# The head of an attention stage: statistics split over two engines, the first pair prepared earlier, input blocks in borrowed memory

## Chip, core and metric

The kernel runs on one core of one Trainium2 chip. The metric is device time in microseconds (us) for one execution; the time before is the median of three runs. TensorE is PE in the profile, VectorE DVE, ScalarE ACT, GpSimd POOL, SyncE SP (it issues nearly all DMAs of the part looked at here).

## The reference, cut to what matters

An image x of 256 x 256 pixels with 128 channels (fp32) goes through two residual layers. Only the first is touched by the change:

```python
def _gn(v, G=32, eps=1e-5):                      # group norm: 32 groups of 4 channels,
    g = v.reshape(B_, H_, W_, G, C_ // G)        # mean and variance over all pixels
    m = jnp.mean(g, axis=(1, 2, 4), keepdims=True)
    s = jnp.var(g, axis=(1, 2, 4), keepdims=True)
    return ((g - m) / jnp.sqrt(s + eps)).reshape(v.shape)

q = split_heads(einsum(_gn(x), wq)) / sqrt(32)   # 4 heads of 32, in each of the 256 rows
k, v = split_heads(einsum(kv_x, wk)), split_heads(einsum(kv_x, wv))
a = softmax(q @ k + bias1 + bias2)
o = (a @ v) * sigmoid(einsum(_gn(x), wg) + bg)
x = x + einsum(o, wo) + bo
# layer 1: x = x + spectral convolutions and attention over channels of _gn(x)
```

The group norm needs all of x before the first query can be made. Keys and values come from kv_x and need no norm.

## The kernel before, in words

The first stage of `layer0` reads x in 32 blocks of 1 MB (`xb`, L129 to L136). A block has 128 partitions of 16 pixels, 128 channels each. PE transposes it in four groups of four 128x128 pieces into a PSUM tile (tag "a", six buffers), and `bn_stats` on DVE writes six numbers per channel and group into `stats`. The blocks have four SBUF buffers, so SP issues the load of block b when PE has read block b - 4. SP's DMAs are issued in program order: a load that has to wait holds all that stand behind it. Eight DMA semaphores are used in turn, so a DMA also waits for the one eight places before it to have landed.

After block 2 come the constants: `gavg` (a matrix that averages 4 channels), `bg`, `adft` and the five weight matrices. These are read through a tile with two buffers (tag "w"), transposed by PE and copied by ACT into `wT`. In SP's program the third weight, `w_wv`, stands behind block 3, and `w_wo` behind block 4. In PE's program the five weight transposes stand between block 2 and block 3. After block 8, `rows.prepare` loads and transposes the two biases (ACT takes the exp, POOL scales it). After the last block, `rows.load(0)` and `rows.load(1)` bring the first two pairs of rows of x and kv_x (`xk`; a pair takes eight DMAs of 64 KB in 128-byte pieces).

Then comes the serial chain. `bn_aggr` (L156) folds all 128 sets of statistics into a mean and a variance per channel, `group_stats` averages over groups with two small matmuls and ends in `rsqrt` (add, ACT's Sqrt, reciprocal and one Newton step), and `rows.fold` scales wq and wg by the norm's factor and makes the biases `qb` and `hbg`.

`rows.run` then does the 256 rows of attention. Its compute and its DMAs are in an order written out by hand, in pairs of rows g: `turn` transposes a pair on DVE (L293), `project` makes queries and keys of a row (PE, then ACT adds `qb`, L308), `values` makes values and the gate's input of a pair, `gates` is the gate's tanh on ACT (L323), `scores` is q times k (L333) and the first two exps (L342), `weigh` multiplies by exp(bias1) on DVE (L354) and POOL (L359) and adds halves on POOL (L364), `attend` applies it to the values. `out` and `spectrum` finish a pair, the latter writing the spectra into U. U is a large SBUF tile, 128 x 129 x 256, allocated from the beginning of the kernel; before the first `spectrum` only its first 2048 elements of a partition are in use, as the landing place of bias1.

Pools are stacked: `rows.run` opens its pools after the first stage's pools have closed, and takes over their SBUF and PSUM.

Of the kernel before, what the change touches and what calls it, by code (L numbers as in the profile page):

```python
# [10 lines left out]
FP = mybir.dt.float32  # L11
AF = mybir.ActivationFunctionType
ALU = mybir.AluOpType
# [83 lines left out]
def layer0(tc, I, C, ident, x1d, U, Q2, mv2, groups):  # L97

    nc = tc.nc
    x = I["x"][0]
    NS = x.shape[0]
    with ExitStack() as ctx:
        const = ctx.enter_context(tc.tile_pool(name="l0c", bufs=1))  # L110
        rctx = ctx.enter_context(ExitStack())
        wT = {}
        mr = const.tile([P, 2], FP, name="mr1")
        bg = const.tile([P, 1], FP, name="bg")

        bad = const.tile([P, 2, 8], FP, name="bad")
        onec = const.tile([P, 1], FP, name="onec")
        nc.vector.memset(onec, 1.0)
        adft = const.tile([P, 2, 129], FP, name="adft")

        rows = Rows(tc, I, rctx, x1d, U, Q2, mv2, wT, bg, adft, bad, ident)
        with tc.tile_pool(name="l0p", bufs=2) as pp, tc.tile_pool(
            name="l0pp", bufs=6, space=PSUM
        ) as ps_p:
            gavg = pp.tile([P, P], FP, name="gavg", bufs=1)
            stats = pp.tile([P, NS // 2, 6], FP, name="stats1", bufs=1)

            xr = x.rearrange("s q c -> (s q) c").rearrange("(b p n) c -> b p n c", p=P, n=16)
            for b in range(xr.shape[0]):  # L129
                xb = pp.tile([P, 16, P], FP, tag="xb", name=f"xb_{b}", bufs=4)  # L130
                nc.sync.dma_start(xb, xr[b])
                for t in range(4):
                    ps = ps_p.tile([P, 512], FP, tag="a", name=f"xps_{b}_{t}")
                    for k in range(4):
                        nc.tensor.transpose(ps[:, k * P : (k + 1) * P], xb[:, 4 * t + k, :], ident)
                    nc.vector.bn_stats(stats[:, b * 4 + t, :], ps)  # L136
                if b == 2:
                    nc.sync.dma_start(gavg, C["gavg"])
                    nc.sync.dma_start(bg, I["L0_conv_bg"].unsqueeze(1))
                    nc.sync.dma_start(adft, C["adft"].rearrange("(j p) f -> p j f", p=P))  # L140
                    for n in ("wq", "wk", "wv", "wg", "wo"):
                        w = pp.tile([P, P], FP, tag="w", name="w_" + n)
                        nc.sync.dma_start(w, I["L0_conv_" + n])
                        ps = ps_p.tile([P, 512], FP, tag="a", name="wps_" + n)
                        nc.tensor.transpose(ps[:, 0:P], w, ident)
                        wT[n] = const.tile([P, P], FP, name="wT_" + n)
                        if n in ("wq", "wo"):
                            nc.scalar.mul(wT[n], ps[:, 0:P], WO_SCALE if n == "wo" else 1.0 / math.sqrt(32.0))
                        else:
                            nc.scalar.copy(wT[n], ps[:, 0:P])  # L150
                if b == 8:
                    rows.prepare(pp, ps_p)
            rows.load(0)
            rows.load(1)
            mv = pp.tile([P, 2], FP, name="mv1", bufs=1)
            nc.vector.bn_aggr(mv, stats.rearrange("p a b -> p (a b)"))  # L156
            g = group_stats(nc, pp, ps_p, mv, gavg, "g1")
            nc.vector.tensor_copy(mr, g)
            rows.fold(ps_p, mr)

        rows.run()
        rctx.close()

        with tc.tile_pool(name="l0f", bufs=1) as fp, tc.tile_pool(
            name="l0fp", bufs=1, space=PSUM
        ) as ps_f, tc.tile_pool(name="l0fg", bufs=1, space=PSUM) as ps_g:
            groups.load(fp)
            f = fp.tile([P, 3], FP, name="f")
# [12 lines left out]
            again = nc.values_load(fi[0:1, 0:1])  # L181
            groups.make(fp, ps_g, mv2, "g2")
            with tc.If(again > 0):
                layer0_general(tc, I, ident, x1d, U, Q2, wT, mr, bg, adft)
                for k in range(8):
                    row_sums(nc, U, Q2, mv2, k)
                groups.make(fp, ps_g, mv2, "g3")
# [9 lines left out]
class Rows:  # L197
# [20 lines left out]
        self.b2T = const.tile([P, 2, self.NS], FP, name="b2T")  # L218
        self.rows, self.raw = {}, {}

    def fold(self, psum, mr):

        nc = self.tc.nc
        nc.vector.tensor_scalar(self.nm, mr[:, 0:1], -1.0, None, ALU.mult)
        ps = psum.tile([P, 512], FP, tag="a", name="foldps")
        for k, n in enumerate(("wq", "wg")):
            nc.vector.tensor_scalar(self.wn[n], self.wT[n], mr[:, 1:2], None, ALU.mult)
            nc.tensor.matmul(ps[:, k : k + 1], self.wn[n], self.nm, start=True, stop=True)
        nc.vector.tensor_copy(self.qb, ps[:, 0:1])
        nc.vector.tensor_scalar(self.hbg, ps[:, 1:2], self.bg, 0.5, ALU.add, ALU.mult)  # L230

    def prepare(self, bp, ps_b):
        nc, I, ident = self.tc.nc, self.I, self.ident
# [36 lines left out]
    def run(self):  # L270
# [1 line left out]
        nc = tc.nc  # L272
        ctx, wT, rows, raw = self.ctx, self.wT, self.rows, self.raw
        b1T, b2T, bad = self.b1T, self.b2T, self.bad
        wk = ctx.enter_context(tc.tile_pool(name="l0wk", bufs=2))
        ps_s = ctx.enter_context(tc.tile_pool(name="l0s", bufs=1, space=PSUM))
        ps_a = ctx.enter_context(tc.tile_pool(name="l0a", bufs=4, space=PSUM))
        pairs = {}
        turned = wk.tile([P, 6, 512], FP, name="turned", bufs=1)

        def by_columns(out, w, src, start=True, stop=True):

            for h in range(4):
                hd = slice(32 * h, 32 * h + 32)
                nc.tensor.matmul(out[hd], w[:, hd], src, start=start, stop=stop)  # L285
# [4 lines left out]
        def turn(g):  # L290
# [6 lines left out]
            if g + 2 < NS // 2:  # L297
                self.load(g + 2)

        def project(s):  # L300
            p, q = row(s)
            ps = ps_a.tile([P, 512], FP, tag="a", name=f"qk_{s}")
            by_columns(ps[:, 0:256], self.wn["wq"], p["xT"][:, q])
            by_columns(ps[:, 256:512], wT["wk"], p["kvT"][:, q])
            r = rows[s] = {}
            r["qkT"] = wk.tile([P, 512], FP, tag="qkT", name=f"qkT_{s}")

            nc.scalar.activation(r["qkT"], ps, AF.Identity, bias=self.qb)  # L308

        def values(g):  # L310
            p = pairs[g]
            ps = ps_a.tile([P, 512], FP, tag="a", name=f"v_{g}")
            for c in range(4):
                by_columns(ps[:, c * P : (c + 1) * P], p["kvT"][:, c * P : (c + 1) * P], wT["wv"])
            p["v"] = wk.tile([P, 4, P], FP, tag="v", name=f"v_{g}")
            nc.scalar.copy(p["v"].rearrange("p c d -> p (c d)"), ps)
            p["g"] = ps_a.tile([P, 512], FP, tag="a", name=f"g_{g}")
            by_columns(p["g"], self.wn["wg"], p["xT"])

# [104 lines left out]
        def whole(k):  # L424
            return 0 <= k < NS // 2

        with tc.manual_schedule(engines={ENG.PE, ENG.Activation, ENG.DVE, ENG.Pool, ENG.SP}):
            turn(0)
            for i in range(-1, NS + 5):
                g, odd = i // 2, i % 2  # L430
                if odd and whole(g - 2):
                    again(g - 2)
                    squares(g - 2)
                if not odd and whole(g):
                    gates(g)
                if 0 <= i < NS:
                    scores(i)
# [2 lines left out]
                if 0 <= i < NS:  # L440
                    exp = rows[i].pop("exp")
                    exp(1, 0)
                    exp(1, 1)
                    weigh(i)
                if odd and whole(g + 1):
                    values(g + 1)
                if odd and whole(g + 2):
                    turn(g + 2)
                if not odd and whole(g - 2):
# [1684 lines left out]
```

## Time and profile before

| | us |
|---|---|
| median of 3 runs | 2658.32 (2653.32 to 2668.18) |
| the profiled execution | 2673.89, span 2672.1 |
| end of the last `bn_stats` in the span | 102.4 |
| first product with exp(bias1) on DVE, on POOL | 122.0, 123.8 |
| the rows of attention | about 123.8 to 1436 |
| layer 1 | the rest, to 2672.1 |

A line of the timeline gives the start, the length, the engine, the line of the kernel, the operation with output and inputs, how many were merged, and in brackets how long the engine sat idle before and what released it. In tables of windows, each engine's busy time stands in the window, then the granted PE clock (1.00 is full), the share of the DMA engines in use, and the bytes moved.

### The profile page before, as it was taken

The page shows a single profiled execution, that of the slowest core. Times are in us where ns is not written, and L with a number is a line of the kernel's source. Part 1 is how long each engine was busy: PE and PEld are TensorE (multiplying, and loading weights), DVE is VectorE, ACT ScalarE, POOL GpSimd, SP SyncE. Part 2 cuts the span into 40 slices and gives each one's busy share as a digit, 9 for nine tenths or more (in the row PEclk, how much of TensorE's full clock was granted, in tenths as well). Part 3 has the DMA queues.
Part 4 walks back from the last instruction along what each step waited for, and adds up shares of the span by engine and source line. Part 5 has one row for each costly group of instructions (what it writes and reads, how often), then busy time and mean ns, then how long its engine had stood idle before and what let it go on. Part 6 is the DMA issues. An engine that isn't in the chain of part 4 may idle for free. (4 is left out here: it accounts for less than half of the span.)

```text
span 2672.1 us, 88760 instructions
## 1 busy us (share of the span) xinstructions
PE 2426.5 (91%) x37572; PEld 1549.0 (58%) x37572; DVE 2027.5 (76%) x2886; ACT 1421.3 (53%) x2718; POOL 1488.8 (56%) x1042
## 2 busy tenths in 40 slices
PE   6699999999999999999997999998979978898754
PEld 6555655555656555565554567786755456444533
DVE  6799999999999999999996457566546654465455
ACT  0278888888888888888884122001016401555232
POOL 1199999999999999999994012002136411111211
PEclk8899999999999999999998989999989988899855
DMA  9755666556566666565652011888877764997598
GB/s 348 222 91 100 107 105 107 101 104 105 105 105 109 107 107 108 102 106 103 109 101 63 4 58 47 274 272 289 297 264 265 239 223 149 332 359 260 192 386 344
DMA packets 1017925, 459.02 MB, mean 172 GB/s; under 512 B 831094, under 2 KB 947273, under 8 KB 1011128
## 3 DMA queue, kind: packets, MB, share of 16 engines
q1 hardware_dynamic: 977720, 363.13, 54.1%
q0 software_dynamic: 22912, 81.80, 7.9%
q10 hardware_dynamic: 16896, 8.39, 1.1%
q8 instruction: 298, 4.88, 0.8%
q14 instruction: 99, 0.81, 0.1%
HBM read 317.89 MB, written 135.27 MB: 170 GB/s over the span
## 5 line engine op out<-in xcount | busy, mean ns | idle before, releaser
L359 POOL TENSOR_TENSOR e<-e,b1T 128x1024 f32<-128x1024 f32 x256 | 607.1, 2372 | 143.8 <-DMA xk<-in_x_dram 76.2
L364 POOL TENSOR_TENSOR es<-e 128x512 f32<-128x512 f32 x512 | 648.4, 1289 | 0.0
L386 DVE RECIPROCAL av<-av 128x256 f32<-128x256 f32 x256 | 452.1, 1766 | 9.1
L342 ACT ACTIVATE sc<-sc,b2T 128x512 f32<-128x512 f32 x512 | 338.7, 662 | 122.9 <-PE sc L333 110.8
L342 ACT ACTIVATE e<-sc,b2T 128x512 f32<-128x512 f32 x512 | 324.7, 694 | 0.0
L354 DVE TENSOR_TENSOR e<-sc,b1T 128x1024 f32<-128x1024 f32 x256 | 310.9, 1215 | 9.7 <-ACT sc L342 9.3
L333 PE MATMUL sc<-qkT 32*128 32x256 f32 x4096 | 293.9, 400 | 3.4 <-DVE e L354 3.4
L1392 PE MATMUL yps<-xt,mpT 128*128 128x256 f32 x1024 | 252.8, 398 | 29.2 <-DVE yt L1404 12.6
L374 PE MATMUL av<-e,v 128*32 128x256 f32 x4096 | 269.1, 379 | 1.8 <-DVE gate L387 1.7
L333 PEld LDWEIGHTS sc<-qkT 32*128 32x128 f32 x4096 | 185.5, 184 | 115.2 <-issue 53.0
L1392 PEld LDWEIGHTS yps<-xt,mpT 128*128 128x128 f32 x1024 | 195.7, 197 | 75.4 <-DVE yt L1404 18.7
L374 PEld LDWEIGHTS av<-e,v 128*32 128x32 f32 x4096 | 130.0, 109 | 126.1 <-issue 38.3
L1408 POOL DMA_DIRECT2D yd<-yt x32 | 17.5, 546 | 320.2 <-DVE yt L1404 317.5
L308 ACT ACTIVATE qkT<-qk,qb 128x512 f32<-128x512 f32 x256 | 174.4, 681 | 7.5 <-PE qk L285 7.5
L285 PEld LDWEIGHTS u<-adft,x 128*32 128x32 f32 x4096 | 120.6, 111 | 82.7 <-issue 78.6
L285 PE MATMUL qk<-turned,wn_wq 128*32 128x256 f32 x2048 | 164.5, 393 | 1.8 <-DVE turned L293 1.8
L410 ACT ACTIVATE turned<-turned 128x256 f32<-128x256 f32 x256 | 104.4, 408 | 113.7 <-DVE x1b L396 111.4
L379 PE MATMUL av<-es,ones 128*32 128x256 f32 x2048 | 161.1, 379 | 1.6 <-POOL es L364 1.6
L285 PE MATMUL qk<-turned,wT_wk 128*32 128x256 f32 x2048 | 158.4, 381 | 0.0
L293 DVE STREAM_TRANSPOSE turned<-xk 128x1024 f32<-128x1024 f32 x128 | 157.9, 1234 | 0.1
L1795 ACT ACTIVATE blocks<-h2ps,col 128x512 f32<-128x512 f32 x128 | 88.9, 777 | 128.3 <-PE h2ps L1259 128.3
L285 PE MATMUL u<-adft,x 128*32 128x129 f32 x4096 | 139.5, 276 | 6.2 <-DMA x<-x1d 6.2
(532 smaller groups left out, 4177.7 us busy)
## 6 DMA issues: line engine op xcount, KB each, us to landing
xt<-x1d SPq DMA_DIRECT2D x128, 512.0 KB, 7.8
xb<-in_x_dram SPq DMA_DIRECT2D x32, 1024.0 KB, 7.8
xk<-in_x_dram SPq DMA_DIRECT2D x512, 64.0 KB, 3.1
xk<-in_L_conv_kv_x_dram SPq DMA_DIRECT2D x512, 64.0 KB, 2.5
x1d<-x1b SPq DMA_DIRECT2D x512, 64.0 KB, 2.2
x<-x1d SPq DMA_DIRECT2D x128, 256.0 KB, 3.2
y<-yd SPq DMA_DIRECT2D x62, 512.0 KB, 6.3
gs<-Gd SPq DMA_DIRECT2D x384, 64.0 KB, 5.3
```

What stands on the lines that cost most here:

```text
L285: nc.tensor.matmul(out[hd], w[:, hd], src, start=start, stop=stop)
L293: nc.vector.transpose(turned[:, a : b + 1 : b - a].rearrange("p k (b c) -> p k b c", c=32), t)
L308: nc.scalar.activation(r["qkT"], ps, AF.Identity, bias=self.qb)
L333: nc.tensor.matmul(sc[h // 2][:, h % 2, c * 256 : (c + 1) * 256], qkT[p, 256 + c * P : 256 + (c + 1) * P], qkT[p, 0:256], start=True, stop ...
L342: nc.scalar.activation(r["e"][1][:, :, c, :] if hp else z, z, AF.Exp, bias=b2T[:, c, s : s + 1])
L354: nc.vector.tensor_tensor(r["e"][0].rearrange("p h c q -> p (h c q)"), r.pop("sc").rearrange("p h x -> p (h x)"), b1T[:, 0:2].rearrange("p ...
L359: nc.gpsimd.tensor_tensor(e1, e1, b1T[:, 2:4].rearrange("p h c q -> p (h c q)"), ALU.mult)
L364: nc.gpsimd.tensor_tensor(es, e[:, :, 0, :], e[:, :, 1, :], ALU.add)
L374: nc.tensor.matmul(ps[hd, 0:256], p["v"][:, 2 * (s % 2) + c, hd], r["e"][h // 2][:, h % 2, c, :], start=(c == 0), stop=(c == 1),)
L379: nc.tensor.matmul(ps[32 * h : 32 * h + 32, 256:512], self.ones, r["es"][h // 2][:, h % 2, :], start=True, stop=True,)
L386: nc.vector.reciprocal(rd, rd)
L1392: nc.tensor.matmul(rows_of(ps[j]), mpT[:, sc, tt], by_turn(xt[:, sc])[:, j], start=(sc == 0), stop=False,)
```

## The change

- `Rows.run` becomes a generator in four steps. Its pool for `turned`, `qkT` and `v` and its PSUM pool of four banks are opened ahead of the first stage, whose PSUM buffers go from six to four.
- The blocks of x land in U (five places behind the bias) instead of a pool with four buffers.
- After block 29, ACT sums the statistics of the first 30 blocks (the means shifted by the first one, their squares, and the second moments) with three activations, and a Sqrt of one column follows on ACT. POOL makes mean and variance of them with six small operations. `gavg` becomes two matrices, weighted by the blocks' shares 30/32 and 2/32, scaled by POOL after block 2.
- `bn_aggr` takes the last two blocks only. The two averaging matmuls become two pairs, accumulating in PSUM. DVE reads PSUM itself where ACT made a copy.
- `turn(0)` and the keys of row 0 stand between the second averaging matmul and `rsqrt`; row 0's query stands between the fold of wq and that of wg. The values of pair 0 follow, and the gate's matmuls and tanh of pair 0 move behind the exps of row 0.
- In every row, the keys' four matmuls now stand ahead of the queries' four.

```diff
         rows = Rows(tc, I, rctx, x1d, U, Q2, mv2, wT, bg, adft, bad, ident)
+        steps = rows.run()
+        next(steps)
         with tc.tile_pool(name="l0p", bufs=2) as pp, tc.tile_pool(
-            name="l0pp", bufs=6, space=PSUM
+            name="l0pp", bufs=4, space=PSUM
         ) as ps_p:
-            gavg = pp.tile([P, P], FP, name="gavg", bufs=1)
+            gavg = pp.tile([P, 2, P], FP, name="gavg", bufs=1)
...
+            room = U.rearrange("p f s -> p (f s)")
...
-                xb = pp.tile([P, 16, P], FP, tag="xb", name=f"xb_{b}", bufs=4)
+                xb = room[:, 2048 * (1 + b % 5) : 2048 * (2 + b % 5)].rearrange("p (n c) -> p n c", c=P)
                 nc.sync.dma_start(xb, xr[b])
...
+                    for k, share in ((1, late / NB), (0, 1 - late / NB)):
+                        nc.gpsimd.tensor_scalar(gavg[:, k], gavg[:, 0], share, None, ALU.mult)
...
+                if b == NB - late - 1:
+                    early = stats[:, 0 : 4 * (b + 1)].rearrange("p b (h k) -> p (b h) k", h=2)
+                    n, flat = 8 * (b + 1), junk[:, 0 : 8 * (b + 1)]
+                    nc.gpsimd.tensor_scalar(col[:, 6:7], early[:, 0, 1:2], -1.0, None, ALU.mult)
+                    nc.scalar.activation(flat, early[:, :, 1], AF.Identity, bias=col[:, 6:7], accum_out=col[:, 7:8])
+                    nc.scalar.activation(
+                        flat, early[:, :, 1], AF.Square, bias=col[:, 6:7], accum_out=col[:, 8:9]
+                    )
+                    nc.scalar.activation(flat, early[:, :, 2], AF.Identity, accum_out=col[:, 9:10])
+                    nc.scalar.activation(col[:, 10:11], col[:, 9:10], AF.Sqrt)
+                    g = nc.gpsimd
+                    g.tensor_scalar(col[:, 7:9], col[:, 7:9], 1.0 / n, None, ALU.mult)
...
             rows.load(0)
             rows.load(1)
-            mv = pp.tile([P, 2], FP, name="mv1", bufs=1)
-            nc.vector.bn_aggr(mv, stats.rearrange("p a b -> p (a b)"))
-            g = group_stats(nc, pp, ps_p, mv, gavg, "g1")
-            nc.vector.tensor_copy(mr, g)
-            rows.fold(ps_p, mr)
-
-        rows.run()
+
+            last = pp.tile([P, 2], FP, name="mv1", bufs=1)
+            with tc.manual_schedule(engines={ENG.PE, ENG.Activation, ENG.DVE, ENG.Pool}):
+                nc.vector.bn_aggr(last, stats[:, 4 * (NB - late) :].rearrange("p a b -> p (a b)"))
+                nc.vector.tensor_copy(col[:, 1:4:2], last)
+                ps = ps_p.tile([P, 512], FP, tag="a", name="g1_ps")
+                for k in range(2):
+                    nc.tensor.matmul(ps[:, 0:1], gavg[:, k], col[:, k : k + 1], start=(k == 0), stop=(k == 1))
+                nc.vector.tensor_copy(mr[:, 0:1], ps[:, 0:1])
+                d = col[:, 4:6]
+                nc.vector.tensor_scalar(d, col[:, 0:2], mr[:, 0:1], None, ALU.subtract)
+                nc.vector.tensor_mul(d, d, d)
+                nc.vector.tensor_add(d, d, col[:, 2:4])
+                ps = ps_p.tile([P, 512], FP, tag="a", name="g1_ps2")
+                for k in range(2):
+                    nc.tensor.matmul(ps[:, 0:1], gavg[:, k], d[:, k : k + 1], start=(k == 0), stop=(k == 1))
+                next(steps)
+                rsqrt(nc, pp, mr[:, 1:2], ps[:, 0:1], EPS, "g1")
+                ps = ps_p.tile([P, 512], FP, tag="a", name="foldps")
+                rows.fold(ps, mr, "wq")
+                next(steps)
+                rows.fold(ps, mr, "wg")
+
+        for _ in steps:
+            pass
...
+        def keys(s):
+            p, q = row(s)
+            ps = ps_a.tile([P, 512], FP, tag="a", name=f"qk_{s}")
+            rows[s] = {"qk": ps}
+            by_columns(ps[:, 256:512], wT["wk"], p["kvT"][:, q])
...
+        yield
+        turn(0)
+        keys(0)
+        yield
+        project(0)
+        yield
+        wk = ctx.enter_context(tc.tile_pool(name="l0wk", bufs=2))
+        ps_s = ctx.enter_context(tc.tile_pool(name="l0s", bufs=1, space=PSUM))
         with tc.manual_schedule(engines={ENG.PE, ENG.Activation, ENG.DVE, ENG.Pool, ENG.SP}):
-            turn(0)
-            for i in range(-1, NS + 5):
+            values(0)
+            turn(1)
+            for i in range(0, NS + 5):
...
+                if i == 0:
+                    gate(0)
+                    gates(0)
```

`fold` now does one of its two weights per call, and `gate` holds the gate's matmuls that `values` had; both are otherwise as before.

More of the change, by code (lines that the diff above doesn't have):

```diff
@@ L121, in layer0 @@
         rows = Rows(tc, I, rctx, x1d, U, Q2, mv2, wT, bg, adft, bad, ident)
+        steps = rows.run()
+        next(steps)
         with tc.tile_pool(name="l0p", bufs=2) as pp, tc.tile_pool(
-            name="l0pp", bufs=6, space=PSUM
+            name="l0pp", bufs=4, space=PSUM
         ) as ps_p:
-            gavg = pp.tile([P, P], FP, name="gavg", bufs=1)
+            gavg = pp.tile([P, 2, P], FP, name="gavg", bufs=1)
             stats = pp.tile([P, NS // 2, 6], FP, name="stats1", bufs=1)
+            col = pp.tile([P, 12], FP, name="col1", bufs=1)
+            junk = pp.tile([P, NS], FP, name="junk1", bufs=1)
+            room = U.rearrange("p f s -> p (f s)")
             xr = x.rearrange("s q c -> (s q) c").rearrange("(b p n) c -> b p n c", p=P, n=16)
-            for b in range(xr.shape[0]):
-                xb = pp.tile([P, 16, P], FP, tag="xb", name=f"xb_{b}", bufs=4)
+            NB, late = xr.shape[0], 2
+            for b in range(NB):
+                xb = room[:, 2048 * (1 + b % 5) : 2048 * (2 + b % 5)].rearrange("p (n c) -> p n c", c=P)
                 nc.sync.dma_start(xb, xr[b])
@@ L137, in layer0 @@
                 if b == 2:
-                    nc.sync.dma_start(gavg, C["gavg"])
+                    nc.sync.dma_start(gavg[:, 0], C["gavg"])
                     nc.sync.dma_start(bg, I["L0_conv_bg"].unsqueeze(1))
@@ L150, in layer0 @@
                             nc.scalar.copy(wT[n], ps[:, 0:P])
+                    for k, share in ((1, late / NB), (0, 1 - late / NB)):
+                        nc.gpsimd.tensor_scalar(gavg[:, k], gavg[:, 0], share, None, ALU.mult)
                 if b == 8:
                     rows.prepare(pp, ps_p)
+                if b == NB - late - 1:
[10 more added lines that the diff above has]
+                    g.tensor_scalar(col[:, 7:9], col[:, 7:9], 1.0 / n, None, ALU.mult)
+                    g.tensor_tensor(col[:, 0:1], col[:, 7:8], col[:, 6:7], ALU.subtract)
+                    g.tensor_tensor(col[:, 7:8], col[:, 7:8], col[:, 7:8], ALU.mult)
+                    g.tensor_scalar(col[:, 9:10], col[:, 9:10], 1.0 / (256 * n), None, ALU.mult)
+                    g.tensor_tensor(col[:, 8:9], col[:, 8:9], col[:, 7:8], ALU.subtract)
+                    g.tensor_tensor(col[:, 2:3], col[:, 8:9], col[:, 9:10], ALU.add)
@@ L219, in __init__, with fold @@
         self.rows, self.raw = {}, {}
-    def fold(self, psum, mr):
+    def fold(self, ps, mr, n):
         nc = self.tc.nc
[L224 to L230, printed above, removed]
+        nc.vector.tensor_scalar(self.wn[n], self.wT[n], mr[:, 1:2], None, ALU.mult)
+        if n == "wq":
+            nc.vector.tensor_scalar(self.nm, mr[:, 0:1], -1.0, None, ALU.mult)
+            nc.tensor.matmul(ps[:, 0:1], self.wn[n], self.nm, start=True, stop=True)
+            nc.vector.tensor_copy(self.qb, ps[:, 0:1])
+        else:
+            nc.tensor.matmul(ps[:, 1:2], self.wn[n], self.nm, start=True, stop=True)
+            nc.vector.tensor_scalar(self.hbg, ps[:, 1:2], self.bg, 0.5, ALU.add, ALU.mult)
     def prepare(self, bp, ps_b):
@@ L274, in run @@
         b1T, b2T, bad = self.b1T, self.b2T, self.bad
-        wk = ctx.enter_context(tc.tile_pool(name="l0wk", bufs=2))
-        ps_s = ctx.enter_context(tc.tile_pool(name="l0s", bufs=1, space=PSUM))
+        first = ctx.enter_context(tc.tile_pool(name="l0w1", bufs=2))
         ps_a = ctx.enter_context(tc.tile_pool(name="l0a", bufs=4, space=PSUM))
         pairs = {}
-        turned = wk.tile([P, 6, 512], FP, name="turned", bufs=1)
+        turned = first.tile([P, 6, 512], FP, name="turned", bufs=1)
         def by_columns(out, w, src, start=True, stop=True):
@@ L298, in turn @@
                 self.load(g + 2)
+        def keys(s):
[3 more added lines that the diff above has]
+            by_columns(ps[:, 256:512], wT["wk"], p["kvT"][:, q])
         def project(s):
             p, q = row(s)
-            ps = ps_a.tile([P, 512], FP, tag="a", name=f"qk_{s}")
+            if s not in rows:
+                keys(s)
+            r = rows[s]
+            ps = r.pop("qk")
             by_columns(ps[:, 0:256], self.wn["wq"], p["xT"][:, q])
-            by_columns(ps[:, 256:512], wT["wk"], p["kvT"][:, q])
-            r = rows[s] = {}
-            r["qkT"] = wk.tile([P, 512], FP, tag="qkT", name=f"qkT_{s}")
+            r["qkT"] = first.tile([P, 512], FP, tag="qkT", name=f"qkT_{s}")
             nc.scalar.activation(r["qkT"], ps, AF.Identity, bias=self.qb)
@@ L314, in values, with gate @@
                 by_columns(ps[:, c * P : (c + 1) * P], p["kvT"][:, c * P : (c + 1) * P], wT["wv"])
-            p["v"] = wk.tile([P, 4, P], FP, tag="v", name=f"v_{g}")
+            p["v"] = first.tile([P, 4, P], FP, tag="v", name=f"v_{g}")
             nc.scalar.copy(p["v"].rearrange("p c d -> p (c d)"), ps)
+        def gate(g):
+            p = pairs[g]
             p["g"] = ps_a.tile([P, 512], FP, tag="a", name=f"g_{g}")
@@ L433, in run @@
                     squares(g - 2)
-                if not odd and whole(g):
+                if not odd and whole(g) and g > 0:
                     gates(g)
@@ L444, in run @@
                     weigh(i)
+                if i == 0:
+                    gate(0)
+                    gates(0)
                 if odd and whole(g + 1):
                     values(g + 1)
+                    gate(g + 1)
                 if odd and whole(g + 2):
```

## The prediction

> **What bounds the kernel now.** First the page, for where the change lies: its last edit acts in the rows of attention, all others before the first POOL product at 123.8 us of the span.
>
> ```profile
> span 2672.1 us, 88760 instructions
> ...
> PE   6699999999999999999997999998979978898754
> ...
> DMA  9755666556566666565652011888877764997598
> ```
>
> A slice is 66.8 us. In slices 3 to 21 PE is at 9 and the DMA at 5 or 6: the rows are bound by engines, and their table of windows (123.8 to 1436) gives PE 1307.9 of 1312.2 us, DVE 1266.7, POOL 1244.1, that is 5.1 us a row. Only the first two slices can get shorter, and the rows just start sooner if their rate stays. Second, the windows of the first stage:
>
> ```profile
> 10.00:15.00 5.00, 3.06 (x25) 2.52 (x23) 4.56 (x8) 0.04 (x1) 0.00 (x0) 1.00 0.75 263
> 15.00:20.00 5.00, 0.83 (x3) 0.35 (x2) 0.00 (x0) 0.95 (x4) 0.00 (x0) 0.54 0.69 242
> ...
> 25.00:30.00 5.00, 5.00 (x45) 5.00 (x44) 4.84 (x8) 0.00 (x0) 0.00 (x0) 0.94 0.82 282
> ...
> 45.00:50.00 5.00, 4.11 (x35) 3.46 (x32) 5.00 (x10) 0.00 (x0) 2.56 (x2) 1.00 0.90 316
> ...
> 60.00:90.00 30.00, 23.50 (x196) 20.87 (x193) 29.99 (x49) 0.00 (x0) 0.00 (x0) 1.00 1.01 420
> ...
> 102.40:123.80 21.40, 9.01 (x102) 6.19 (x104) 9.67 (x20) 8.02 (x13) 0.00 (x0) 0.68 0.37 59
> ```
>
> From 60 to 90 us the DMA share is 1.01 at 420 GB/s: the stage is bound by loading, 2.48 us per block, and DVE (four `bn_stats` starting 0.60 apart, 2.40 us per block) follows closely. Before that the DMA has holes: at 420 GB/s the windows at 10, 15, 25 and 45 lack 1.9, 2.1, 1.6 and 1.2 us of transfer. In the last row, between the last statistic and the first POOL product, no engine is busy for half of the time: a serial chain. Third, the timeline, for what makes the holes and for the chain:
>
> ```profile
> 14.96 0.33 SPq L143 DMA_DIRECT2D w_wv<-in_L_conv_wv_dram  x1
> ...
> 21.17 0.45 PE L145 MATMUL wps_wo<-ident,w_wo 128*128 128x128 f32 x1 [2.99 <-DMA w_wo<-in_L_conv_wo_dram]
> ...
> 22.51 0.70 DVE L136 BATCH_NORM_STATS2 stats<-xps 128x6 f32<-128x512 f32 x1 [7.95 <-PE xps L135]
> ...
> 43.96 2.49 DVE L136 BATCH_NORM_STATS2 stats<-xps 128x6 f32<-128x512 f32 x4 [5.59 <-PE xps L135]
> ...
> 99.94 2.49 DVE L136 BATCH_NORM_STATS2 stats<-xps 128x6 f32<-128x512 f32 x4 [1.09 <-PE xps L135]
> ...
> 102.47 3.62 DVE L156 BATCH_NORM_AGGREGATE mv<-stats 128x2 f32<-128x768 f32 x1
> ...
> 106.23 0.56 PE L50 MATMUL g_ps<-mv,gavg 128*128 128x1 f32 x2 [5.02 <-DVE mv L156]
> ...
> 108.48 1.28 ACT L37 ACT_TABLE_LOAD   x1
> ...
> 112.70 0.16 DVE L229 COPY qb<-foldps 128x1 f32<-128x1 f32 x1 [0.97 <-PE foldps L228]
> ...
> 113.08 2.37 DVE L293 STREAM_TRANSPOSE turned<-xk 128x1024 f32<-128x1024 f32 x2
> ...
> 116.51 0.69 ACT L308 ACTIVATE qkT<-qk,qb 128x512 f32<-128x512 f32 x1 [6.53 <-PE qk L285]
> ...
> 118.68 1.28 ACT L323 ACT_TABLE_LOAD   x1
> ...
> 118.80 1.15 PE L333 MATMUL sc<-qkT 32*128 32x256 f32 x16
> ...
> 120.56 1.35 ACT L342 ACTIVATE sc<-sc,b2T 128x512 f32<-128x512 f32 x2
> ...
> 122.00 1.23 DVE L354 TENSOR_TENSOR e<-sc,b1T 128x1024 f32<-128x1024 f32 x1 [6.55 <-ACT sc L342]
> ```
>
> `w_wv` waits for the transpose of `w_wq`, which lands late; block 4 stands behind it, DVE sits idle 7.95 us, and the DMA runs dry. Call the end of the last statistic T0: 102.43. From T0 on: the exp starts at +18.13, DVE's product at +19.57, POOL's at +21.38.
>
> **Part 1: blocks in U, five places (T0 moves).** The order of SP's instructions shows blocks 3 and 4 both ahead of `w_wv`. Block 4 waits only for block 1 (landed at 8.14), so it follows block 3 (landed 17.22) and lands at 19.7 instead of 20.87. `w_wv`, still issued at 15.0, now lands behind it (20.0 instead of 17.5); `w_wo` goes out at 20.5 behind block 5 and lands at 22.7 instead of 21.03, and PE takes block 3 up 1.6 us later. But blocks 5, 6 and 7 need no buffer back, and land at 22.5, 25.2, 27.6 where they came at 23.5, 26.0, 32.2. Block 8 waits for PE to read block 3, as block 7 did (issue 25.06): 26.5, landing 5 us later (block 4's latency on an idle queue was 5.06), 31.5 instead of 35.08. The bias and block 9 took 7.6 us behind block 8: 39.1 instead of 42.70. DVE then starts block 9 at 40.9 instead of 43.96, because the bias transposes now wait for PSUM (four buffers, not six). Blocks 10 to 31 are 22 x 2.48 = 54.6, plus 1.1 for the last, which took 3.58 us with the first `xk` pieces behind it: 94.8 instead of 99.14. DVE needs 22 x 2.40 from 40.9, 93.7, so the DMA still ends last. T0 moves from 102.4 to 97.9: **-4.5 us**. Bounds: -2.5, if stalls of a kind I have not seen take back two (the bias loads' 2.76 us issue of `b2n` sits there), to -6, if the last block loses its 1.1 and blocks 10 to 15, which lost 0.7, run clean.
>
> Four PSUM buffers in place of six cost nothing else: PE makes a tile in 0.44 us, DVE takes 0.60.
>
> **Part 2: the chain from T0.** `bn_aggr` took 3.62 us for 768 elements and 1.89 for 384 (another line), so 48 take 0.38. Copy +0.63. The second averaging matmul +0.74 to +1.30 (0.56; its first half is done beforehand). DVE reads it itself, three small operations at 0.2: +2.09. Two matmuls, 0.98 as the folds' pair: +3.18. `turn(0)` runs meanwhile, +2.13 to +3.36 (1.23). Its data: the last piece landed 3.2 us after the last block, T0 - 0.1, so no wait. `rsqrt`: add +3.55, Sqrt at once (0.20) because its table was loaded early, reciprocal to Newton's end +4.76 by the same steps as 110.01 to 110.95. `wn_wq` +5.07, fold +5.74, `qb` +5.94. Query matmuls to +6.7 (1.08), ACT's `qkT` +6.75 to +7.44. PE in between: the fold of wg and the 30 remaining value matmuls (1.87 at the granted 0.5), to +9.0. Scores +9.0 to +10.2. ACT copies v to +9.65 and loads the exp table to +10.95: the exp starts at +10.95 where it was +18.13, since tanh no longer stands first. DVE's product +12.4, ACT's second exps to +14.3, POOL +14.4 where it was +21.38. The gate's tanh (0.69) falls between +14.3 and the next scores' end at +15.2. **-7.0 us**.
>
> What was added and hidden: three ACT sums of 240 elements (0.41 for 256, plus 0.19 for reading the accumulator: 1.8), the load 1.28 and Sqrt 0.20, together 3.3 us; POOL's six operations by the nearest rows between 0.19 (copy of 128x1) and 0.76 (128x256), taken at 0.3, the row of the same width being 0.19, ready 3 to 6 us after block 29's end. Needed 5.7 after it, when two more blocks (4.96) and 0.74 have passed. Bounds 0 and +0.5; without that cover it would be all of 3 us. POOL's two scalings of `gavg` fall before 40 us, where POOL is idle. The pair loads and `turn(1)` keep their order.
>
> Against it stands the PE clock: the chain's windows were granted 0.5 from 104 to 117.8 and full from there, 3.4 us after dense work began, so the scores ran warm in 1.15. Now dense work begins at about +5.2. Cold, the 16 would take 0.85 more (eight query matmuls took 1.08 cold and 0.64 warm), to +11.0: just what the table load covers. The next row can lose as much; I keep 0 to +1 for the range. The Trainium skill (TensorE: Matmul & The Clock Gate, Part 1) says that the clock falls after an idle window of about 3.4 us and rises after as long a busy one, counted freely from any start; by it the scores at +9.0 would most likely be cold, and the sum of the parts between -11.5 and -10.5. Of the table switch it says (ScalarE: Activation LUTs, What ACT_TABLE_LOAD costs) 1283 ns and a drain of 1380 behind it. The row gives the load but no drain: 108.48 plus 1.28, and Sqrt begins at 109.78. By that page taking the load out would be worth another 1.4 us and the sum -12.9; the row decides.
>
> **Part 3: keys before queries.** The same eight matmuls, 2032 each at 379 to 403 ns, one ACT reader waiting for all: 0.
>
> Sum: -4.5 - 7.0 = -11.5 us on the profiled 2673.9, giving 2662.4. That execution lay 15.6 above the median of 2658.3, so the median becomes 2647, 0.43% less. About 0.5%, 13.3 us, is what a measurement of this kernel can tell from no change.
>
> **Rivals.** (a) T0 stays: the DMA is the bound from 35 us on, and the later `w_wo` gives back what block 4 won. Against: the holes at 25 and 45 go in any case. Then -7, 2651. (b) Both parts at their good ends: T0 -6 or more, the chain -7.5: -14, 2644; for it, the holes sum to 6.8 us. (c) Slower: the new order in the rows. PE has 0.3% idle there, so a bubble when the query's weights follow the keys' is paid 256 times; the head's gain is gone from 0.045 us a row, and from 0.097 it is slower by over 0.5%: at 0.11, 2675. Against: the weights' load rows are 109 and 110 ns in either place, with the same waits. (d) The early sums are late: ACT's or POOL's small operations three times as dear, +2 to +3 on the chain: -9, 2649.
>
> **How the numbers follow.** Forecast 0.52, (a) 0.18, (b) 0.20, (c) 0.05, (d) 0.05. Three runs spread over 15 us, so a median is good to some 5: below 2645 falls a third of the forecast, most of (b) and little else, 0.34; above 2671.6 (c) and a stray, 0.05; the rest 0.61. The range 2637 to 2657 takes in (a), (b) and (d) with that spread and leaves (c) out.
>
> **What would show it.** Right: block 9's first statistic near 41, the last one's end near 98, no table load between it and the fold, POOL's first product 14 to 15 us after it, rows at 5.1 us. Part 1 is wrong if the last statistic stays above 100; Part 2 if `turn(0)` waits for a DMA, if PE's first averaging matmul waits for POOL, or if the scores start later than +10. Row time over 5.2 us would be (c), and would make the whole wrong.

## The result and the profile after

| us | before | after |
|---|---|---|
| median of 22 runs each | 2664.74 (2652.13 to 2675.12) | 2655.36 (2644.42 to 2666.84) |
| the profiled execution, its span | 2673.89, 2672.1 | 2647.98, 2646.2 |
| end of the last `bn_stats` (T0) | 102.43 | 99.95 |
| POOL's first product | 123.81 | 115.12 |
| from there to POOL's last product | 1306.90 | 1305.78 |
| the rest, layer 1 | 1241.42 | 1225.27 |

The ratio of after to before is 0.9964, with the interval [0.9952, 0.9976]: 9.6 us less, between 6.4 and 12.8. The interval excludes no change, though the difference is smaller than the 0.5% that the prediction names as what can be told from none. With 22 runs the median of before itself came out 6.4 above that of the first three.

The two profiled spans differ by 25.9 us, and this must not be read as the gain: 16.1 of it lie in layer 1, which the change doesn't touch, and whose length scattered between 1225 and 1242 us over the profiled executions below. Nor are the 1.1 us by which the rows are shorter the work of the change: in the trace of before the granted clock stood at 0.50 once more, from 124.6 to 128.0 us, and the second row took 5.99 us instead of 5.0, while the run with five places alone below, with the old chain and the old order, has rows of 1305.84. What is left is the way to POOL's first product: 8.7 us less in this pair of traces. The page shows PE denser in the first two slices and the rest nearly as it was:

```profile
span 2646.2 us, 88789 instructions
...
PE   7899999999999999999997999998979978888754
...
DMA  9755565656656665656562011888978764997599
```

The windows of the first stage (columns as before: engines, granted PE clock, DMA share, GB/s: the last column is a rate), then the chain from T0 to POOL's first product, then the rows:

```profile
10.00:15.00 5.00, 4.24 (x32) 3.72 (x30) 4.70 (x9) 0.19 (x1) 1.09 (x2) 1.00 0.99 366
15.00:20.00 5.00, 0.10 (x1) 0.13 (x1) 0.40 (x1) 0.29 (x2) 0.00 (x0) 0.78 0.92 341
20.00:25.00 5.00, 2.60 (x12) 2.29 (x13) 0.70 (x1) 0.76 (x3) 0.00 (x0) 0.50 0.62 241
25.00:30.00 5.00, 5.00 (x34) 5.00 (x33) 4.38 (x7) 0.00 (x0) 0.00 (x0) 0.70 0.84 331
...
45.00:50.00 5.00, 3.88 (x32) 3.46 (x32) 5.00 (x10) 0.00 (x0) 0.66 (x1) 1.00 1.01 416
...
60.00:85.00 25.00, 19.38 (x160) 17.32 (x160) 24.83 (x41) 0.00 (x0) 0.00 (x0) 1.00 1.02 422
99.95:115.10 15.15, 12.01 (x106) 6.52 (x106) 6.72 (x20) 6.03 (x10) 0.00 (x0) 0.66 0.61 97
115.10:1427.30 1312.20, 1306.47 (x24380) 778.80 (x24380) 1267.51 (x1429) 1071.66 (x2162) 1243.23 (x768) 1.00 0.59 103
```

The holes at 10, 15 and 45 us have shrunk (263, 242 and 316 GB/s are now 366, 341 and 416), but new ones stand at 20 and 30 us: 241 and 302 GB/s, where before had 414 and 345. The bound of 2.48 us a block is unchanged from 60 us on, and in the rows every engine's busy time is within 0.11% of what it was. The timeline:

```profile
5.62 2.81 SPq L137 DMA_DIRECT2D U<-in_x_dram  x2
...
14.80 0.33 SPq L149 DMA_DIRECT2D w_wv<-in_L_conv_wv_dram  x1
...
20.38 0.33 SPq L149 DMA_DIRECT2D w_wo<-in_L_conv_wo_dram  x1
...
24.30 0.70 DVE L142 BATCH_NORM_STATS2 stats<-xps 128x6 f32<-128x512 f32 x1 [8.90 <-PE xps L141]
...
41.44 0.70 DVE L142 BATCH_NORM_STATS2 stats<-xps 128x6 f32<-128x512 f32 x1 [1.61 <-PE xps L141]
...
95.60 1.28 ACT L170 ACT_TABLE_LOAD   x1
...
96.89 0.20 ACT L170 ACTIVATE col<-col 128x1 f32<-128x1 f32 x1
...
97.46 2.49 DVE L142 BATCH_NORM_STATS2 stats<-xps 128x6 f32<-128x512 f32 x4 [1.61 <-PE xps L141]
97.49 0.19 POOL L177 TENSOR_TENSOR col<-col 128x1 f32<-128x1 f32 x1
...
99.98 0.37 DVE L183 BATCH_NORM_AGGREGATE mv<-stats 128x2 f32<-128x48 f32 x1
...
102.23 1.25 DVE L336 STREAM_TRANSPOSE turned<-xk 128x1024 f32<-128x1024 f32 x1 [0.24 <-DMA xk<-in_L_conv_kv_x_dram]
...
106.89 0.69 ACT L358 ACTIVATE qkT<-qk,qb 128x512 f32<-128x512 f32 x1 [3.13 <-PE qk L328]
...
109.12 2.09 PE L386 MATMUL sc<-qkT 32*128 32x256 f32 x16
...
109.85 1.28 ACT L395 ACT_TABLE_LOAD   x1
...
111.25 1.36 ACT L395 ACTIVATE sc<-sc,b2T 128x512 f32<-128x512 f32 x2
...
112.64 1.23 DVE L407 TENSOR_TENSOR e<-sc,b1T 128x1024 f32<-128x1024 f32 x1 [3.65 <-ACT sc L395]
...
113.15 0.69 ACT L358 ACTIVATE qkT<-qk,qb 128x512 f32<-128x512 f32 x1 [0.54 <-PE qk L328]
...
115.12 2.37 POOL L412 TENSOR_TENSOR e<-e,b1T 128x1024 f32<-128x1024 f32 x1 [17.44 <-ACT e L395]
```

Blocks 3 and 4 go out one behind the other from 5.62 on, ahead of `w_wv`; `w_wo` goes out 2.4 us later than before, and block 3 is taken up 1.8 us later. Yet block 9 follows with 1.61 us of idle DVE in place of 5.59. ACT's and POOL's early sums end at 97.7, 2.9 us ahead of their use at 100.6. `bn_aggr` takes 0.37 in place of 3.62, and the wait of 0.24 ahead of `turn(0)`, put down to a DMA, is no wait: in eight traces, with eight different T0, it is the same 0.24. The scores took 2.09 at a granted clock of 0.50, where they took 1.15 before, and end at 111.21, when the table load has just ended (111.13).

T0 in the six profiled executions whose first stage is that of the changed kernel (this one, and five of the experiments below) is 99.95, 99.98, 99.41, 99.12, 99.79 and 99.25: mean 99.58, 2.85 us less than before (of the kernel before there is one trace, and the six lie 0.9 apart, so this is good to about 1 us). The chain from T0 to POOL's first product is 21.38, 21.46 and 21.08 us where its code is the old one, and 15.17, 14.57, 14.65, 14.44 and 14.44 where it is the changed one: means 21.31 and 14.65, 6.65 us less. Together 9.5 us, which fits the 9.6 of the medians.

### The profile page after: what moved, and what is told of

It reads as the page before. It is cut to its first block, busy times and chain, and to the rows that moved or that the text cites. A ratio compares the mean times of both kernels' runs of the same rounds, so it can differ in the third digit from the quotient of the medians.

```text
span 2646.2 us, 88789 instructions
## 1 busy us (share of the span) xinstructions
PE 2417.9 (91%) x37576; PEld 1542.8 (58%) x37576; DVE 2025.1 (77%) x2887; ACT 1421.6 (54%) x2723; POOL 1490.0 (56%) x1051
## 5 line engine op out<-in xcount | busy, mean ns | idle before, releaser
L1458 PEld LDWEIGHTS yps<-xt,mpT 128*128 128x128 f32 x1024 | 193.5, 194 | 71.8 <-DVE yt L1470 17.5
L328 PE MATMUL qk<-turned,wT_wk 128*32 128x256 f32 x2048 | 164.5, 393 | 0.8 <-DVE g_ve L35 0.8
L328 PE MATMUL qk<-turned,wn_wq 128*32 128x256 f32 x2048 | 158.3, 381 | 0.0
```

The lines of the kernel that those rows point to most:

```text
L1458: nc.tensor.matmul(rows_of(ps[j]), mpT[:, sc, tt], by_turn(xt[:, sc])[:, j], start=(sc == 0), stop=False,)
```

## The experiments

Each run is read by four markers in its trace: T0, the distance from T0 to POOL's first product ("chain"), the rows, and the time. Single times scatter by 10 us and decide nothing here; the markers do, each run being one execution unless more are named. Edits are against the changed kernel unless said otherwise.

**Blocks in U alone.** The kernel before, with only this edit:

```diff
-                xb = pp.tile([P, 16, P], FP, tag="xb", name=f"xb_{b}", bufs=4)
+                xb = room[:, 2048 * (1 + b % 5) : 2048 * (2 + b % 5)].rearrange("p (n c) -> p n c", c=P)
```

> The kernel before, with one edit: the blocks of x land in U, in five places. PSUM keeps six buffers and the chain is the old one. My theory (the fifth place lets SP send a block before PE has freed one): the last statistic ends at 98.5 to 100 us of the span instead of 102.4, the chain from there to POOL's first product stays at 21.4. Rival (block 4 standing ahead of the third weight in SP's order is what moved it; here it stands behind): it stays at 102 or above.

Measured: T0 98.32, chain 21.46, rows 1305.84; 2665.48 us, and 2665.44 for one execution of the kernel before beside it. Its timeline:

```profile
5.48 0.33 SPq L132 DMA_DIRECT2D U<-in_x_dram  x1
...
17.94 7.14 SPq L132 DMA_DIRECT2D U<-in_x_dram  x4
...
22.20 0.70 DVE L137 BATCH_NORM_STATS2 stats<-xps 128x6 f32<-128x512 f32 x1 [7.54 <-PE xps L136]
```

Only one block stands ahead of `w_wv`: block 4 is still behind it, five places or not. What the fifth place does is further on: blocks 5, 6 and 7 go out in a row, and block 7 lands at 28.17 in place of 32.20. That alone brings T0 to 98.32, 0.2 us below what I expected, and 0.8 to 1.7 us earlier than in the six traces of the whole change. The rows' order of queries and keys is still the old one, and their length the same.

**Four places in U.**

```diff
-                xb = room[:, 2048 * (1 + b % 5) : 2048 * (2 + b % 5)].rearrange("p (n c) -> p n c", c=P)
+                xb = room[:, 2048 * (1 + b % 4) : 2048 * (2 + b % 4)].rearrange("p (n c) -> p n c", c=P)
```

> The changed kernel with four places in U instead of five, all else as changed. My theory: the last statistic returns to 102 or later (it ended at 99.95 with five), the chain to POOL's first product stays at 15.2. Rival (memory or PSUM buffers moved it): it stays at about 100.

Measured: T0 99.10, chain 14.57, rows 1305.87, 2652.63 us. My theory missed: without the fifth place T0 is as early as with it (99.1 to 100.0). Block 4 still went out ahead of `w_wv`, at 9.39 when block 0 had been read, and the loads of `bo` and of the first bias moved ahead of blocks 7 and 8. So something else in the change sets SP's order.

**Four PSUM buffers alone.** The kernel before, with only this edit:

```diff
-            name="l0pp", bufs=6, space=PSUM
+            name="l0pp", bufs=4, space=PSUM
```

> The kernel before with one edit: four PSUM buffers in the first stage instead of six. Blocks keep their own four SBUF buffers. With this number the scheduler puts block 4 ahead of the third weight and the biases ahead of blocks 7 and 8 in SP's order, as it did with four places in U. New theory (the order of SP's loads, which the PSUM buffers decide, is what moved the last statistic): it ends at 98.8 to 100 us instead of 102.4, the chain stays at 21.4. Rival (the blocks' place in U matters in itself): 102 or later.

Measured: T0 100.14, chain 21.08, 2663.37 us.

```profile
5.71 4.00 SPq L131 DMA_DIRECT2D xb<-in_x_dram  x2
...
14.77 0.33 SPq L143 DMA_DIRECT2D w_wv<-in_L_conv_wv_dram  x1
...
24.05 0.70 DVE L136 BATCH_NORM_STATS2 stats<-xps 128x6 f32<-128x512 f32 x1 [9.19 <-PE xps L135]
```

Two blocks now go out ahead of `w_wv`, in the kernel before, with its own four buffers. It is the number of PSUM buffers that puts block 4 there, and `bo` and the first bias ahead of blocks 7 and 8; T0 comes 2.3 us earlier with it, 0.1 later than I expected. (That a scheduler which reckons with the PSUM tiles does it is the likely way; the run shows only that the order follows the number. That the 2.3 us come from the order, and not from the number in some other way, is argued, not shown.) The two edits don't add up: alone -4.1 and -2.3, together -2.85, since the PSUM cut also lets `w_wo` and block 3 come later (24.05 and 24.30 in place of 22.51, against 22.20 with five places alone).

**The weights' stall taken away.** Five buffers for the weights, and then also ten places for the blocks:

```diff
-                        w = pp.tile([P, P], FP, tag="w", name="w_" + n)
+                        w = pp.tile([P, P], FP, tag="w", name="w_" + n, bufs=5)
```

> The changed kernel with five buffers for the weights' tile in place of two, so that no weight waits for PE. My theory (a stall of SP behind the third and fifth weight leaves holes in the DMA from 20 to 30 us, 3.2 us of transfer): block 3 goes to PE near 18 instead of 23, and the last statistic ends at 96.5 to 98 instead of 99.95. Rival (the DMA is the bound and the order of transfers makes no difference): 99.5 to 100.5.

```diff
-                xb = room[:, 2048 * (1 + b % 5) : 2048 * (2 + b % 5)].rearrange("p (n c) -> p n c", c=P)
+                xb = room[:, 2048 * (1 + b % 10) : 2048 * (2 + b % 10)].rearrange("p (n c) -> p n c", c=P)
```

> As the one with five weight buffers, with ten places for blocks in U. My theory: no block waits for PE in the first 40 us, the holes are gone, and the last statistic ends at 95.5 to 97. Rival (the bias's small pieces and the last block's delay are what is left, and places do not help): the same as with five places within 0.5.

Measured: T0 97.85 and 96.63, chain 14.65 and 14.44, 2655.19 and 2655.02 us. Both as expected. In the first of the two:

```profile
5.56 0.33 SPq L149 DMA_DIRECT2D w_wv<-in_L_conv_wv_dram  x1
...
10.66 0.33 SPq L149 DMA_DIRECT2D w_wo<-in_L_conv_wo_dram  x1
...
18.17 0.70 DVE L142 BATCH_NORM_STATS2 stats<-xps 128x6 f32<-128x512 f32 x1 [3.34 <-PE xps L141]
```

`w_wo` is under way at 10.7 in place of 20.4, and DVE idles 3.34 us in place of 8.90. With these runs a rule for T0 shows. Add up what each window of 5 us from 5 to 60 lacks to 420 GB/s:

| kernel | holes, us | T0 |
|---|---|---|
| before | 9.1 | 102.43 |
| before, four PSUM buffers | 7.1 | 100.14 |
| changed | 6.2 | 99.95 |
| before, five places in U | 5.4 | 98.32 |
| changed, five weight buffers | 3.1 | 97.85 |
| changed, that and ten places | 2.6 | 96.63 |

T0 less the holes is 92.9 to 94.8 in all six, while T0 itself moves by 5.8; over all fourteen traces it is 92.3 to 94.8. The load is the bound of this stage, and an edit there is worth about the DMA time that it fills. The rule is good to some 1 us and no finer: from the changed kernel to five places alone the holes fall by 0.8 and T0 by 1.6, and four places have slightly more holes than the changed kernel (6.5) and an earlier T0. Nor is every hole idle time: before, from 30 to 35 us, the DMA share was 0.98 at 345 GB/s.

**The first pairs' loads held back.** A write to the first pair's tile that reads the last block makes its DMAs wait for that block:

```diff
-            rows.load(0)
+            rows.load(0, xb[:, 0:2, 0:1])
...
+        if behind is not None:
+            nc.gpsimd.tensor_scalar(t[:, :, 0, 0:1], behind, 0.0, None, ALU.mult)
```

> The changed kernel with the first pair's loads held back until the last block of x has landed (POOL writes one column of their tile, reading that block). My theory (the 128-byte pieces behind it slow the last block, 4.10 us for 2.48): the last block lands 2.5 us after the one ahead, the last statistic ends 1.5 us earlier, near 98.4, and turn(0) now waits for its data some 3 us. Rival (it is slow for another reason): the last statistic stays at 100.

Measured: T0 97.68, chain 16.48, rows 1311.36, 2663.19 us. The last block lands 2.79 us after the one before it (one load of the second pair, 64 KB, still went out right behind it). It takes 4.10 in the changed kernel and 3.3 to 3.9 in the twelve other traces, all with the first pair's pieces behind it: the pieces of 128 bytes do slow it, by 0.5 to 1.3 us. The rest of the earlier T0 is not due to this edit: block 9 had already landed at 39.25, and at 40.1 to 40.8 in the six traces of the changed first stage. And the pair now comes late:

```profile
95.19 2.49 DVE L142 BATCH_NORM_STATS2 stats<-xps 128x6 f32<-128x512 f32 x4 [0.30 <-PE xps L141]
...
101.89 1.25 DVE L338 STREAM_TRANSPOSE turned<-xk 128x1024 f32<-128x1024 f32 x1 [2.17 <-DMA xk<-in_x_dram]
```

`turn(0)` now does wait for a DMA, 2.17 us, starting at T0 + 4.21 in place of + 2.28. POOL's first product comes at 114.15, between the 115.12 and 113.69 of two executions of the changed kernel: no gain shows.

**The whole `bn_aggr` put back.** The split over two engines is undone (one `bn_aggr` over all statistics, single averaging matmuls, no sums on ACT and POOL; the early Sqrt stays, on a column of the statistics):

```diff
-                nc.vector.bn_aggr(last, stats[:, 4 * (NB - late) :].rearrange("p a b -> p (a b)"))
+                nc.vector.bn_aggr(last, stats.rearrange("p a b -> p (a b)"))
...
-                    nc.tensor.matmul(ps[:, 0:1], gavg[:, k], d[:, k : k + 1], start=(k == 0), stop=(k == 1))
+                nc.tensor.matmul(ps[:, 0:1], gavg[:, 0], d[:, 0:1], start=True, stop=True)
```

> The changed kernel without the early sums on ACT and POOL: bn_aggr takes all 32 blocks and one averaging matmul each stands where two stood; the early Sqrt stays. My theory: the split is worth bn_aggr's 3.62 less 0.37, so POOL's first product comes 18.4 us after the last statistic instead of 15.2. Rival (turn's data, which landed 2.2 us after the last statistic, sets the chain, and part of the 3.2 is covered): 16.5 to 17.5.

Measured: T0 99.98, `turn(0)` at + 5.62, chain 17.59, rows 1307.01, 2651.99 us. `turn(0)` came 3.3 us later, as much as `bn_aggr` is longer (3.62 to 0.37), but POOL's product only 2.4 to 3.2 later than where the chain is the changed one, mean 2.9: less than the 18.4 expected, and hardly more than the rival's 17.5. PE's clock was up when this kernel's scores ran, and that gave part of it back:

```profile
111.80 1.15 PE L367 MATMUL sc<-qkT 32*128 32x256 f32 x16 [0.16 <-ACT qkT L339]
```

**Turn and keys behind the fold.**

```diff
-                next(steps)
                 rsqrt(nc, pp, mr[:, 1:2], ps[:, 0:1], EPS, "g1")
                 ps = ps_p.tile([P, 512], FP, tag="a", name="foldps")
                 rows.fold(ps, mr, "wq")
-                next(steps)
                 rows.fold(ps, mr, "wg")
+                next(steps)
+                next(steps)
```

> The changed kernel with turn(0) and the keys of row 0 behind both folds, where they stood before. My theory: turn's 1.25 and the keys' 1.08 come back onto the chain, with the folds ahead of the query some 2.8 us: POOL's first product 17.5 to 18 us after the last statistic instead of 15.2. Rival (the value matmuls and the exp table load bound it anyway): under 16.

Measured: T0 99.41, `turn(0)` at + 7.12, chain 17.28, rows 1305.86, 2656.16 us. The early turn and keys are worth 2.1 to 2.8 us, mean 2.6, a little less than expected; the scores took 1.31 here, partly warm. If the two add up, which no run tests, they are with the 2.9 of the split 5.5 of the 6.65 us; the rest (DVE's reading of PSUM, the table ready early, tanh behind the exps) wasn't taken apart.

**Without the early Sqrt.**

```diff
-                    nc.scalar.activation(col[:, 10:11], col[:, 9:10], AF.Sqrt)
```

> The changed kernel without the Sqrt of one column behind the early sums. My theory (an ACT table load waits for nothing but the instruction ahead of it): the load stands behind the last early sum all the same, and POOL's first product stays 15.2 us after the last statistic. Rival (the load waits with the Sqrt that needs it): 16.4, or 17.8 with a drain behind it.

Measured: T0 99.12, chain 13.24, rows 1309.70, 2655.99 us.

```profile
95.39 1.28 ACT L37 ACT_TABLE_LOAD   x1
...
102.72 0.20 ACT L37 ACTIVATE g_r<-g_ve 128x1 f32<-128x1 f32 x1 [6.05 <-DVE g_ve L35]
...
103.55 1.91 PE L327 MATMUL v<-wT_wv,turned 128*32 128x128 f32 x26
...
107.29 1.15 PE L385 MATMUL sc<-qkT 32*128 32x256 f32 x16
```

The load came as my theory had it, the chain did not: 13.24 where 15.2 was expected. Two things show. The table load ran at 95.39, as soon as ACT's last sum was done, 7.3 us ahead of the Sqrt that needed it: here it waited for the instruction before it on ACT and for nothing else. In the kernel before that instruction was the copy of the second average, so the load was exposed; since DVE makes this copy, the early Sqrt isn't needed. And the greater part of the value matmuls (26 of 32) now stood ahead of the fold, where PE otherwise idles, and PE had its full clock in time for the scores, which took 1.15 us.

**The values moved by hand.** To hold the second apart, three of the four parts of the values are put behind the keys of row 0, and the early Sqrt is left out:

```diff
         keys(0)
+        multiply(0, range(3))
         yield
```

> The changed kernel with 12 of the 16 value matmuls of pair 0 written ahead of the norm's rsqrt, and without the early Sqrt. Theory (in the run without the early Sqrt, 13 of them stood ahead of the fold by the scheduler's doing; PE worked through the gap and its clock was up when the scores came): POOL's first product comes 13.0 to 13.6 us after the last statistic instead of 15.2, the scores take 1.15 and not 2.09. Rival (that run's clock window just fell well): 14.5 to 15.2.

Measured: T0 99.79, chain 13.24, rows 1305.78, 2651.57 us. As expected, the scores took 1.15 us, and the chain is 1.2 to 1.9 us shorter than in the changed kernel's two executions. The windows of this run, and beneath them the same ones of the changed kernel:

```profile
103.00:106.00 3.00, 2.63 (x34) 1.75 (x34) 1.50 (x9) 0.20 (x1) 0.00 (x0) 0.50 0.42 67
106.00:109.00 3.00, 2.85 (x35) 1.77 (x34) 1.69 (x4) 1.75 (x3) 0.00 (x0) 0.93 0.73 117
```

```profile
103.00:106.00 3.00, 2.23 (x16) 1.26 (x20) 1.82 (x11) 0.20 (x1) 0.00 (x0) 0.51 0.39 62
106.00:109.00 3.00, 3.00 (x40) 1.87 (x32) 1.67 (x4) 0.69 (x1) 0.00 (x0) 0.50 0.75 119
```

PE's clock is full from about 106.4 here, and from about 113.3 there. This doesn't rule out the rival, that the clock's window fell well in this run too: the next experiment has the values in the same place and a cold clock.

**All together, beside the changed kernel again.** Five weight buffers, ten places, values first, no early Sqrt, and an early Exp behind the Sqrt that takes the second table load off the chain:

```diff
                 rsqrt(nc, pp, mr[:, 1:2], ps[:, 0:1], EPS, "g1")
+                nc.scalar.activation(col[:, 10:11], col[:, 9:10], AF.Exp)
```

> The changed kernel with five weight buffers, ten places in U, 12 value matmuls ahead of rsqrt, no early Sqrt, and an Exp of one column behind rsqrt's Sqrt, so that the exp table is loaded before the query is there. Theory: last statistic at 96.6 to 97.2, POOL's first product 12.3 to 13.0 behind it, at 109 to 110 of the span (115.1 in the changed kernel, 123.8 before), and the median 14 us below the kernel before, a ratio of 0.9945 to 0.995. Rival (the time of layer 1 scatters more than this): no telling it from the changed kernel's 0.9964.

> The changed kernel once more, beside the combined one. Theory: the last statistic at 99 to 100, POOL's first product 15.2 behind it, ratio 0.996 to 0.997.

Measured, 12 runs each: all together 2653.87 us (2641.62 to 2661.26), ratio to the kernel before 0.9953 [0.9935, 0.9971]; the changed kernel 2655.62 us, ratio 0.9969 [0.9955, 0.9984]. The intervals overlap, so the two are not told apart by time, though POOL's first product comes at 111.31 in the one trace and at 113.69 in the other. T0 was 96.94 as expected; the chain was 14.37, not 12.3 to 13.0, and my theory missed there:

```profile
100.76 1.28 ACT L197 ACT_TABLE_LOAD   x1
101.37 1.91 PE L328 MATMUL v<-wT_wv,turned 128*32 128x128 f32 x26
...
105.83 2.09 PE L395 MATMUL sc<-qkT 32*128 32x256 f32 x16
...
107.96 1.36 ACT L404 ACTIVATE sc<-sc,b2T 128x512 f32<-128x512 f32 x2 [1.41 <-PE sc L395]
```

The exp's table is loaded at 102.0, off the chain. But the scores ran cold although the values stand first, and so the exp waits 1.41 us for PE where it used to wait for the table. Over all traces, 26 of the 32 value matmuls stood ahead of the fold in four, and the scores took 1.15 us in three of them and 2.09 in this one; where two stood ahead, in six, they took 1.73 to 2.09. So values first makes a warm clock likelier, no more. The changed kernel's second execution gave chain 14.44, not the 15.2 expected, and rows 1305.78.

## Why the prediction was right, and where not

The sum of -11.5 us stands beside -9.5 by the traces and -9.6 by the ratio. The forecast of 2647 lies 8.4 under the median of 2655.4: 6.4 of this is the level (three runs of before against 22), 2 the sum. The median lies within the range of 2637 to 2657 by only 1.6 us, and three runs of before that lay 2 us lower would have put it outside; that much is luck.

**Part 1, -4.5 forecast, -2.85 measured.** Of the signs that were named, block 9's first statistic came (41.44, near 41). The last one's end near 98 did not: at 99.95 it stands just short of the 100 above which Part 1 was to be wrong, and the six traces go from 99.12 to 99.98. That filled holes would move T0 was right. Two errors stand in it. The cause was half wrong: I read that block 4 goes ahead of `w_wv` in SP's new order and put it under the five places; the four-places run and the PSUM run show that the cut from six PSUM buffers to four does it, which I had costed at nothing beyond a wait of the bias transposes. And in the profiled execution the terms fell short by 2.05 us one after the other: the bias loads and block 9 took 8.5 us behind block 8, not 7.6 (with 0.2 that block 8 was late, 1.1), blocks 10 to 30 took 2.492 each, not 2.48 (0.25), the last one 4.10 instead of 3.58 (0.5; 3.49 in the second execution, so this is scatter), and from its landing to T0 it was 3.29 instead of 3.1 (0.2).

**Part 2, -7.0 forecast, -6.65 measured.** Every step came in its order: `turn(0)` + 2.28 for + 2.13, `qkT` + 6.94 for + 6.75, scores + 9.17 for + 9.0, exp + 11.30 for + 10.95, POOL + 15.17 for + 14.4 in the profiled execution and + 14.44 in the next. What differs between these two is the clock, which rose at 113.3 in the one and at 109.9 in the other: of the 0.73 us, 0.54 are ACT's wait for cold query matmuls of row 1 in front of the exps that POOL waits for, and 0.11 are longer scores. The prediction also read the clock of before as full from 117.8 on; it fell once more, from 124.6 to 128.0 (section on the result). The cold scores cost 0.94 us where 0.85 was forecast, and the table load covered it; where that cover went, in the kernel with all edits, the cost showed as a wait of 1.41 us. The early sums were hidden as forecast: done at 97.7, needed at 100.6.

The Trainium skill (TensorE: Matmul & The Clock Gate, Part 1) was the better guide on this clock: the scores were cold, as the prediction drew from it, and a window that runs freely fits a kernel that shows 14.44 once and 15.17 once. That the clock rises after one busy window, the kernel with all edits does not bear out (last section). On the table load (ScalarE: Activation LUTs, What ACT_TABLE_LOAD costs) the 1283 ns agree with every row, and the drain of 1380 ns doesn't show: 95.60 plus 1.28, and the Sqrt begins at 96.89.

**Part 3, 0 forecast, 0 measured.** Whichever matmuls stand first take 391 ns and the others 379. The groups of the rows in the changed kernel:

```profile
L328 PE MATMUL qk<-turned,wT_wk 128*32 128x256 f32 x2032 | 162.4, 391 | 0.0
...
L328 PE MATMUL qk<-turned,wn_wq 128*32 128x256 f32 x2032 | 156.2, 379 | 0.0
```

and in the run with five places alone, in the old order:

```profile
L286 PE MATMUL qk<-turned,wn_wq 128*32 128x256 f32 x2032 | 162.3, 391 | 0.0
...
L286 PE MATMUL qk<-turned,wT_wk 128*32 128x256 f32 x2032 | 156.2, 379 | 0.0
```

The numbers change places, and the rows take 1305.78 and 1305.84 us.

**The rivals.** (a) falls: T0 moved, though less than with five places alone, where `w_wo` wasn't late; that a later `w_wo` gives something back, as (a) said, fits this. (b) falls: neither part reached its good end. (c) falls by the rows. (d) falls by POOL's last sum, 97.7.

In three single executions (without the early Sqrt, with the late pairs, with four PSUM buffers alone) all rows took 1309.7 to 1312.7 us in place of 1305.8. Their traces tell where: some rows, mostly every fourth in a stretch, are up to 2.3 us longer, and there DVE's transpose of the pair's result (`x1b`) waits for the DMA that writes an earlier one out (`x1d<-x1b`): 8 waits of 7.9 us in sum, 16 of 12.6 and 9 of 9.2, against one of 0.3 us in the other eleven traces together. Two things stay open: why those writes landed late in these three, and layer 1's scatter of 17 us, which is larger than the whole gain and is why the combined kernel's 2.4 us can't be seen in its median.

## What to carry to other kernels

Where loading bounds a stage, sum the holes of the DMA against its full rate, and price each edit by the hole that it fills; ask of every buffer count, in PSUM too, whether a scheduler will order the loads anew for it. A serial chain behind a reduction is shortened by what can be done before the last input (partial statistics) and by what doesn't depend on it (keys, values, table loads); then look for what is late next, here PE's clock. A gain of some microseconds in 2650 is read from markers in several traces, not from two spans.

## What had not been expected of the hardware

- A table load ran as soon as the instruction before it on ACT was done, 7.3 us ahead of the activation that needed it.
- PE's clock rose after very different times of nearly unbroken work: with the values first, about 3 us after 103.4; in the kernel with all edits, busy in every microsecond from 101 on, not before 108.6. The stretch at half clock lasted 3.4 us in the first, 6.8 and 10.2 in the two executions of the changed kernel, 10.2 with all edits and 13.7 before (104.1 to 117.8): whole multiples of 3.4. That is the window that the Trainium skill gives (TensorE: Matmul & The Clock Gate, Part 1), but by it one busy window is enough, and the 7.6 us of the kernel with all edits are longer than two.
- `bn_aggr` takes 0.37 us for 48 elements, 1.89 for 384 and 3.62 for 768; POOL's smallest operations take 0.19 to 0.23.
- What stands behind a large transfer matters: a block of 1 MB takes 2.48 us with more blocks behind it, 2.79 with one load of 64 KB in pieces of 128 bytes, and 3.3 to 4.1 with several of them.
